# Turning edge keys by products with scaled unit matrices, and taking weight parts off in PSUM

## The chip, the cores and the metric

The kernel runs on one core of a Trainium2 chip. The metric is the device time of one execution in microseconds (us); the time shown for a version is the median of its runs.

A core has five engines with instruction queues of their own: TensorE (PE: matrix products, with PEld for loading the stationary operand), VectorE (DVE), ScalarE (ACT), GpSimd (POOL) and SyncE (SP). Here SP starts most transfers and POOL the indirect ones.

## The reference

The input is a graph of 2048 nodes with 256 features and 67584 weighted edges, sorted by dst. First a sparse product is added to x, then a layer of experts:

```python
edge_index = jnp.stack([src, dst])
x = x + _L0_gnn_ref(_layernorm(x, axis=-1), edge_weight, edge_index, node_vec1)
x = x + _L0_ffn_ref(_layernorm(x, axis=-1)[None], Wr, br, ln_g, ln_b, W1, b1, W2, b2)[0]
# _L0_gnn_ref(x, values, indices, bias):
row, col = indices[0], indices[1]                  # src, dst
gathered = values[:, None] * x[col]
return jax.ops.segment_sum(gathered, row, num_segments=2048) + bias
```

`_L0_ffn_ref` routes each token to the best two of 8 experts (256 to 1024 to 256, exact GELU) and adds their results with the softmax weights. All of it is float32.

## The kernel before

**Edge stage (0 to about 216 us).** The adjacency matrix is built densely, transposed, as 16 column blocks, and multiplied with the normalized x. The 2048 dst nodes are cut into 1024 groups of two (`GC = 2`); 128 groups, one on each partition, are a *set*, and there are 8 sets (`GQ`). For each group the kernel finds where its edges begin (`count_before`, `find_blocks`) and loads a window of 128 edges: `win_s` (src), `win_d` (dst) and `win_w` (weight), by three indirect transfers of POOL in `get_win`. In a window the group lies on the partition and the edge in the row. The products need it turned, so each set has a key step:

- `low_key` (L260) on DVE: `b_i` = src >> 7 and `f[:, 0]` = src - 128 * b_i, the src within its block of 128.
- `scale_dst` (L270) on ACT: `cl` = 16 * (dst - first dst of the group). `keys_of` (L275) on DVE adds: `f[:, 1]` = cl + b_i. This second key names a dst of the group and a block of src in a number from 0 to 31; edges of other groups fall outside it.
- `turn_key` (L280): PE transposes one key into a third of the PSUM tile `pk` (one buffer), ACT copies it as bf16, each value twice, to `k2`. It is done for key 0 and for key 1. `turn_weights` (L288) does it for the weights, whose bf16 copy is the first part of `w2`.
- `next_part` (L307), twice a set: DVE subtracts the last part of the weight from what was left (`r`), ACT copies that as bf16 to the next place of `w2`. Three bf16 parts together stand for an f32 weight.
- `count_own` on ACT counts the edges that were covered.

Each set is then worked off in four *half-batches* of 32 groups; there are 32 of them, n = 0 to 31. For half-batch n DVE makes the one-hot matrices: `make_hl` (hl, 128 wide, from key 0), `make_eq` and `make_hr` (eq, 32 wide, from key 1, and hr = eq times the three weight parts). `make_cols` (L345) makes 96 bf16 products of them on PE into `pa` (three PSUM buffers), ACT copies two tiles `ar` out, SP writes them to DRAM and, after every second half-batch, loads a column block `ac` back. From n = 8 on, `dense` (L368) multiplies finished column blocks with xn on PE, and `add` on DVE adds the result to `acc` one half-batch later. In between stands the layer norm of x (`turn_x`, `weigh_x` on PE for n up to 8, the rest on ACT).

The whole stage is in a block whose order is written out by hand for every engine: each engine executes its instructions in the order of the program text. For half-batch n this order is (L483 on): hot matrices of n + 1 on DVE, with `next_part` of a new set around them where n = 2 or n % 4 == 2; `count_before` on ACT; the keys of set q + 1 on DVE (for n = 1 and n % 4 == 0); `get_win`; adds; `make_cols(n)`; `dense`; `turn_keys`; `scale_dst`; `weigh_x`, `turn_x`; work on x. The buffers of hl and hr are two, so DVE can write those of n + 1 only when PE has finished half-batch n - 1. `k2` and `w2` have three buffers, `prep`'s tiles (b_i, f, cl, r1, r2) two.

The constants at the beginning (L112 on) stand outside that block; a scheduler places them.

**Expert stage (216 us to the end).** A branch at L588 closes the edge stage. Then come routing and slots of 256 rows through the experts, mostly on PE, and the copy of the result to the output.

Of the kernel before, what the change touches and what calls it, by code (L numbers as in the profile page):

```python
# [10 lines left out]
F32 = mybir.dt.float32  # L11
BF16 = mybir.dt.bfloat16
F16 = mybir.dt.float16
I32 = mybir.dt.int32
AF = mybir.ActivationFunctionType
OP = mybir.AluOpType
# [6 lines left out]
P = 128  # L23
# [4 lines left out]
def kernel(  # L28
# [30 lines left out]
    nc = tc.nc  # L59
# [26 lines left out]
    NU = NF + NE  # L86
    DX = D + NE
    RW = D + 4
    AHEAD = 2
    EARLY = 3  # L90

    consts = ctx.enter_context(tc.tile_pool(name="consts", bufs=1))
# [71 lines left out]
    nc.vector.memset(ones, 1.0)  # L164
    iota_b = consts.tile([P, P], BF16, name="iota_b")
    nc.vector.tensor_copy(iota_b, iota_p)
    jp = consts.tile([P, P], I32, name="jp")
    nc.gpsimd.iota(jp, pattern=[[1, P]], base=0, channel_multiplier=-1)
    before = consts.tile([P, P], BF16, name="before")
# [30 lines left out]
    wins = [None] * GQ  # L200
# [18 lines left out]
    def get_run(q):  # L219
        runs[q] = find.tile([P, EJ], I32, name="run", bufs=3)  # L220
        nc.gpsimd.indirect_dma_start(
            out=runs[q],
            out_offset=None,
            in_=dst.rearrange("(p j) -> p j", p=P),
            in_offset=bass.IndirectOffsetOnAxis(ap=blk_i[:, q:q + 1], axis=0),
        )
# [33 lines left out]
    def low_key(q):  # L260


        b_i = prep.tile([P, P], I32, name="b_i")
        nc.vector.tensor_scalar(b_i, wins[q][0], 7, None, op0=OP.arith_shift_right)
        f = prep.tile([P, 2, P], F32, name="f")
        nc.vector.scalar_tensor_tensor(f[:, 0, :], b_i, -float(P), wins[q][0], op0=OP.mult,
                                       op1=OP.add)
        return b_i, f

    def scale_dst(q):  # L270
        cls[q] = prep.tile([P, P], F32, name="cl")
        nc.scalar.activation(cls[q], wins[q][1], AF.Identity, bias=col16[:, q:q + 1],
                             scale=float(NB))

    def keys_of(q):  # L275
        b_i, f = low_key(q)
        nc.vector.tensor_tensor(f[:, 1, :], cls[q], b_i, OP.add)
        return f

    def turn_key(q, f, i):  # L280
        if i == 0:
            parts[q] = (keys.tile([P, 2, P, 2], BF16, name="k2"), None,
                        ps_k.tile([P, 3, P], F32, name="pk"))
        k2, _, pk = parts[q]
        nc.tensor.transpose(pk[:, i, :], f[:, i, :], ident)
        nc.scalar.copy(k2[:, i], pk[:, i, :, None].to_broadcast([P, P, 2]))

    def turn_weights(q):  # L288
# [18 lines left out]
    def next_part(q, i):  # L307

        k2, w2, rest = parts[q]
        r = prep.tile([P, P], F32, name=f"r{i}")  # L310
        nc.vector.tensor_tensor(r, rest, w2[:, :, i - 1, 0], OP.subtract)
        nc.scalar.copy(w2[:, :, i, :], r[:, :, None].to_broadcast([P, P, 2]))
        parts[q] = (k2, w2, r)

# [68 lines left out]
    with tc.manual_schedule(engines=ALL):  # L383
# [7 lines left out]
        def turn_x(j):  # L391

            t = ps_s.tile([P, 2, 512], F32, name="py1")
            pt = t[:, 0, :].rearrange("p (b r) -> p b r", r=P)
            for i in range(2 * KD):
                b, k = 2 * j + i // KD, i % KD
                nc.tensor.transpose(pt[:, i, :], acc[:, b, k * P:(k + 1) * P], ident)
            xT = prep.tile([P, 2 * KD, P], F32, name="xT")
            nc.scalar.copy(xT, pt)  # L399
            turned[j] = xT, t  # L400
# [55 lines left out]
        get_run(1)  # L456
        get_run(2)
        get_run(3)
        scale_dst(0)
        b_i, f = low_key(0)  # L460
        turn_key(0, f, 0)
        nc.vector.tensor_tensor(f[:, 1, :], cls[0], b_i, OP.add)
        turn_key(0, f, 1)
        hl = make_hl(0)
        turn_weights(0)
        next_part(0, 1)
# [16 lines left out]
        for n in range(NH):  # L483
            q = n // 4
            new = 1 if n == 2 else q + 1 if n > 4 and n % 4 == 2 and q + 1 < GQ else None
            if n + 1 < NH:
                hl = make_hl(n + 1)
                if new is not None:
                    next_part(new, 1)
                hots[n + 1] = hl, make_hr(n + 1, make_eq(n + 1))  # L490
                if new is not None:
                    next_part(new, 2)
            f = None
            if n == 1:
                fq = 1
                f = keys_of(1)
            if n % 4 == 0 and q + 2 < GQ:
                count_before(q + 2)
            if n % 4 == 0 and q and q + 1 < GQ:
                fq = q + 1  # L500
                f = keys_of(fq)
            elif n % 4 == 1 and q + 2 < GQ:
                get_win(q + 2)
                if q + 4 < GQ:
                    get_run(q + 4)
            if n in (5, 8, 11, 14):
                b = 4 * (n // 3 - 1)
                scales_x(slice(b, b + 4))
            if n in (7, 10, 12, 14):
                b = {7: 0, 10: 4, 12: 8, 14: 12}[n]  # L510
                weigh_n(slice(b, b + 4))
            for p in late:
                add(*p)
            late = []
            make_cols(n, *hots.pop(n))
            g, k = divmod(n - NB // 2, NB // 2)
            if g >= 0:
                late.append(dense(GROUPS[g], 2 * k))
            if f is not None:
                turn_keys(fq, f)  # L520
            if n == 0:

                tr = ps_k.tile([P, 3, P], F32, name="pk").rearrange("p a b -> p (a b)")
                nt = NE * KH + 2 * NE * KD + NB
                cols = consts.tile([P, nt], F32, name="cols")
                o = 0
                for rows in (b1_rows, g_rows, be_rows, nv_rows):
                    m = rows.shape[0]
                    nc.tensor.transpose(tr[:, o:o + m], rows, ident[:m, :m])
                    o += m  # L530
                for k in range(KD):
                    nc.tensor.matmul(tr[:, nt:nt + NE], ones, wr_sb[:, k, :], start=(k == 0),
                                     stop=(k == KD - 1))
                nc.scalar.copy(cols, tr[:, :nt])
                nv_c = cols[:, NE * (KH + 2 * KD):]
                by_e = consts.tile([P, NE, KH + 2 * KD], F32, name="by_e")
                o = 0
                for lo, m in ((0, KH), (KH, KD), (KH + KD, KD)):
                    nc.vector.tensor_copy(by_e[:, :, lo:lo + m],
                                          cols[:, o:o + NE * m].rearrange("p (e n) -> p e n", n=m))  # L540
                    o += NE * m
                nc.sync.dma_start(cols_d.rearrange("e p c -> p e c"), by_e)

                wc = consts.tile([P, KD, NE + 1], F32, name="wc")
                nc.vector.memset(wc[:, :, NE:], 1.0)
                nc.vector.scalar_tensor_tensor(
                    wc[:, :, :NE], tr[:, None, nt:nt + NE].to_broadcast([P, KD, NE]), -1.0 / D, wr_sb,
                    op0=OP.mult, op1=OP.add)
            if n % 4 == 3 and q + 2 < GQ:
                scale_dst(q + 2)  # L550
            if n == 0:
                scale_dst(1)
            if 1 <= n < 9:
                weigh_x(n - 1)
            if n < 8:
                turn_x(n)
            for m, work, j in X_WORK:
                if m == n:
                    work(j)
            if n == 12:  # L560

                less_m = small.tile([P, NB], F32, name="less_m", bufs=1)
                nc.vector.tensor_tensor(less_m, less, nv_c, OP.subtract)
                nc.sync.dma_start(xr_d[N:, :].rearrange("(t p) c -> p t c", p=P),
                                  none[:, None, :].to_broadcast([P, TT, RW]))
                nc.sync.dma_start(y_d[N:, :].rearrange("(t p) d -> p t d", p=P),
                                  none[:, None, :D].to_broadcast([P, TT, D]))
            if n == NH - 3:
                used = small.tile([P, 1], F32, name="used", bufs=1)
                nc.vector.tensor_reduce(used, used_q, AX.X, OP.add)  # L570
                used_i = small.tile([1, 1], I32, name="used_i", bufs=1)
                pu = ps_k.tile([P, 3, P], F32, name="pk")[:, 0, :1]
                nc.tensor.matmul(pu, ones, used, start=True, stop=True)
                nc.vector.tensor_copy(used_i, pu[0:1, :])
# [624 lines left out]
```

## Time and profile before

| | |
|---|---|
| median of 3 runs | 511.28 us (511.26 to 512.25) |
| profiled execution | 512.25 us, its span 510.5 us |
| PE busy | 462.3 us (91%) |
| PEld busy | 394.0 us (77%) |
| DVE busy | 278.2 us (54%) |
| ACT busy | 200.4 us (39%) |
| POOL busy | 154.7 us (30%) |
| hl (L320) on DVE | 32 of 2285 ns |
| hr (L335) on DVE | 32 of 1758 ns |
| products into pa (L359) on PE | 3072, 61.3 us |
| dense products (L373) on PE | 512, 121.3 us |

The profile shows one execution. Its span runs from the first to the last instruction. Products on PE overlap, so the length of one says less than the distance of two starts. A profile line of a single instruction has its start and its length in us, engine, line, operation, output and inputs with their shape, and in brackets how long the engine stood idle before it and what it waited for. PEclk is the clock that TensorE was granted, 1.00 for full speed.

### The profile page before, as it was taken

What the parts mean: (1) busy time and instruction counts of PE and PEld (TensorE: products, weight loads), DVE (VectorE), ACT (ScalarE), POOL (GpSimd) and SP (SyncE); (2) the same over time, 40 slices, a digit from 0 to 9 for tenths busy, and PEclk for the clock granted to TensorE, in tenths of its full rate; (3) what the DMA queues carried; (4) which work ended last, traced back from release to release, by engine and by line L of the source; (5) the groups of instructions that cost most, each with busy time, mean ns of one, the idle gap of its engine ahead of it and who ended that gap; (6) DMA issues with size and microseconds to landing.
All of it is one profiled execution on the core that took longest, in us unless ns stands there. A gap on an engine that the chain in (4) does not pass through costs nothing.

```text
span 510.5 us, 12148 instructions
## 1 busy us (share of the span) xinstructions
PE 462.3 (91%) x4996; PEld 394.0 (77%) x4996; DVE 278.2 (54%) x575; ACT 200.4 (39%) x489; POOL 154.7 (30%) x127
## 2 busy tenths in 40 slices
PE   1669989898999999899999999999999999996993
PEld 0557877676787887788878888888888888886882
DVE  5879899999999984347656122334332222121011
ACT  2355768662433221058272333332333333332220
POOL 5650506133040000000342433554334334422221
PEclk9999789999999999999999999999999999999898
DMA  3755577777656665991514996799998767739421
GB/s 111 221 166 163 189 219 239 219 215 242 212 172 190 202 183 172 346 322 67 163 41 104 342 339 173 233 347 365 349 342 263 208 157 205 217 90 319 139 88 35
DMA packets 87684, 106.82 MB, mean 209 GB/s; under 512 B 8656, under 2 KB 77376, under 8 KB 85504
## 3 DMA queue, kind: packets, MB, share of 16 engines
q1 hardware_dynamic: 79632, 92.08, 55.1%
q0 software_dynamic: 7952, 13.77, 11.3%
q8 instruction: 44, 0.72, 0.6%
q14 instruction: 24, 0.20, 0.1%
q10 hardware_dynamic: 32, 0.04, 0.0%
HBM read 79.85 MB, written 28.14 MB: 212 GB/s over the span
## 4 chain that ended last, share of the span: by engine, by line
PE 43%; DMA 10%; issue 2%; DVE 1%; SPq 0%; POOL 0%; POOLq 0%; ACT 0%; DVEq 0%
PE py L1030 18%; PE ph L1016 17%; DMA xs<-xr_d,to_i 7%; PE py L373 4%; PE px L843 2%; DMA out<-y_d 2%; PE px L981 1%; DMA y_rows<-out,to_i 1%; DMA out<-ys,to_i 0%; PE listed L824 0%; SPq L1168 0%; POOL out L1051 0%; POOLq L1195 0%; DVE in_hi L816 0%; DVE in_lo L810 0%
## 5 line engine op out<-in xcount | busy, mean ns | idle before, releaser
L1016 PE MATMUL ph<-xeT,w 128*128 128x256 f32 (+1 forms) x576 | 123.7, 371 | 5.6 <-PEq L1156 4.0
L1016 PEld LDWEIGHTS ph<-xeT,w 128*128 128x128 f32 x576 | 105.0, 192 | 20.3 <-issue 6.3
L1030 PE MATMUL py<-w,hT 128*128 128x256 f32 x544 | 120.6, 379 | 0.0
L1018 ACT ACTIVATE hT<-ph,ec 128x256 f32<-128x256 f32 (+1 forms) x144 | 65.9, 462 | 137.0 <-PE ph L1016 73.9
L1030 PEld LDWEIGHTS py<-w,hT 128*128 128x128 f32 x544 | 102.0, 190 | 13.2
L373 PE MATMUL py<-xn_lo,ac 128*128 128x264 f32 x352 | 85.1, 394 | 0.0
L1038 POOL DMA_INDIRECT y_d<-ys,to_i x30 | 48.9, 1631 | 114.7 <-DVE ys L1033 80.8
L320 DVE TENSOR_TENSOR hl<-k,iota_b 128x4096 bf16<-128x4096 bf16 x32 | 73.1, 2285 | 4.4 <-PE pa L359 2.2
L373 PEld LDWEIGHTS py<-xn_lo,ac 128*128 128x128 f32 x352 | 65.2, 191 | 12.5 <-ACT ar L362 0.2
L359 PE MATMUL pa<-hl,hr 128*32 128x128 bf16 x3072 | 61.3, 241 | 10.1 <-DVE hr L335 5.6
L359 PEld LDWEIGHTS <-hr 128*32 128x32 bf16 x3072 | 52.5, 108 | 21.7 <-issue 13.3
L1033 DVE SCALAR_TENSOR_TENSOR ys<-py,wt,b2w 128x256 f32<-128x256 f32 x34 | 16.4, 483 | 80.2 <-PE py L1030 65.6
L948 POOL DMA_INDIRECT xs<-xr_d,to_i x40 | 41.9, 1047 | 52.5 <-DVE r L714 32.8
L335 DVE TENSOR_TENSOR hr<-eq,w 128x3072 bf16<-128x3072 bf16 x32 | 56.3, 1758 | 2.5 <-ACT xT L399 0.5
L990 DVE TENSOR_SCALAR xeT<-px,ec 128x256 f32<-128x256 f32 (+1 forms) x38 | 18.4, 526 | 62.9 <-PE px L981 55.3
L362 ACT COPY ar<-pa 128x512 f32<-128x512 f32 x64 | 35.6, 585 | 31.7 <-PE pa L359 22.2
L240 POOL DMA_INDIRECT win_s<-in_src,at_i x8 | 11.3, 1418 | 87.9 <-DVE at_i L236 70.4
L378 DVE TENSOR_TENSOR acc<-acc,py 128x528 f32<-128x528 f32 x37 | 25.8, 700 | 22.2 <-PE py L373 22.2
L373 PE MATMUL py<-xn_hi,ac 128*128 128x264 f32 x160 | 36.2, 387 | 1.4 <-DVEq L588 1.4
L373 PEld LDWEIGHTS py<-xn_hi,ac 128*128 128x128 f32 x160 | 30.2, 190 | 6.8 <-issue 1.8
L1005 ACT ACTIVATE b2w<-b,wt 128x256 f32<-128x256 f32 x36 | 16.3, 500 | 27.9 <-DVE wt L1003 25.6
L327 DVE TENSOR_TENSOR eq<-k,iota_b 128x1024 bf16<-128x1024 bf16 x32 | 21.9, 683 | 0.0
(205 smaller groups left out, 336.3 us busy)
## 6 DMA issues: line engine op xcount, KB each, us to landing
w<-in_L_ffn_W SPq DMA_DIRECT2D x44, 1024.0 KB
ad<-ar SPq DMA_DIRECT2D x32, 512.0 KB
ac<-ad SPq DMA_DIRECT2D x16, 1024.0 KB
b<-in_L_ffn_b SPq DMA_DIRECT2D x22, 128.0 KB
acc<-in_x SPq DMA_DIRECT2D x4, 512.0 KB
out<-y_d SPq DMA_DIRECT2D x4, 512.0 KB
xr_d<-rec SPq DMA_DIRECT2D x1, 1300.0 KB
y_d<-acc SPq DMA_DIRECT2D x1, 1280.0 KB
```

Of the source, the lines that this page charges most:

```text
L320: nc.vector.tensor_tensor(hl.rearrange("p g (n t) -> p g n t", t=2), two(k2[:, 0], g, P), pair(P), OP.is_equal)
L327: nc.vector.tensor_tensor(eq.rearrange("p g (n t) -> p g n t", t=2), two(k2[:, 1], g, RK), pair(RK), OP.is_equal)
L335: nc.vector.tensor_tensor(hr.rearrange("p g i (n t) -> p (g i) n t", t=2), eq[:, :, None, :].to_broadcast([P, GH, 3, RK]), w[:, :, None, : ...
L359: nc.tensor.matmul(pa[j * RK:(j + 1) * RK, m, :], hr[:, g, i, :], hl[:, g, :], start=(i == 0), stop=(i == 2), tile_position=(0, j * RK))
L362: nc.scalar.copy(ar[:, m0:m0 + 4, :], pa)
L373: nc.tensor.matmul(pa[:, i, :DX], acs[c][:, b + i, :], xn(c), start=(c == blocks[0]), stop=(c == blocks[-1]))
L378: nc.vector.tensor_add(acc[:, b:b + 2, :], acc[:, b:b + 2, :], pa[:, :, :DX])
L948: nc.gpsimd.indirect_dma_start(out=(sets[s.set][0] if into is None else into)[:, t, :], out_offset=None, in_=(xr_d if rows is None else ro ...
L1016: nc.tensor.matmul(ph, w1[:, k, c * P:(c + 1) * P], xeT[:, k, :], start=(k == 0), stop=(k == KD - 1))
L1018: nc.scalar.activation(hT[:, c, :s.n * P], ph, AF.Gelu, bias=ec[:, c:c + 1], scale=1.0)
L1030: nc.tensor.matmul(py, hT[:, c, t * P:(t + 1) * P], w2[:, c, :], start=(c == 0), stop=(c == KH - 1))
L1038: st = nc.gpsimd.indirect_dma_start(out=y_d[:, :], out_offset=bass.IndirectOffsetOnAxis(ap=tos[s.to][:, t:t + 1], axis=0), in_=ys, in_offs ...
```

## The change

The low key becomes src & 127, cast to f16 as `lo` (by DVE for set 0, by ACT for the others). ACT makes f16 copies of src (`s_h`) and of the scaled dst (`cl`). DVE no longer computes b_i or either sum. Instead of transposing, PE multiplies the f16 tiles with `turns`, three unit matrices scaled by 1, 1/128 and -1/128, which turns and scales at once: key 0 is lo turned; key 1 is cl + s_h / 128 - lo / 128, three products added up in PSUM.

For sets 0 to 3 (`q < SOON`), `next_part` builds what is left of the weight in PSUM: it turns the window of weights again by an f32 product with the unit matrix and takes off the earlier parts by products with -1 times a unit matrix (`less_b`). DVE's subtraction goes, ACT's copy stays and reads PSUM. For sets 1 to 3 the two calls move in the program: the first after `make_cols(n)`, the second after `turn_x(n)`. Sets 4 to 7 keep the subtraction on DVE. In `turn_key` the order of ACT's work for set 0 changes too: key 0 is copied out before `scale_dst`.

```diff
+    SOON = 4
...
+    turns = consts.tile([P, 3, P], F16, name="turns")
+    for i, c in enumerate((1.0, 1.0 / P, -1.0 / P)):
+        nc.vector.tensor_scalar(turns[:, i, :], ident, c, None, op0=OP.mult)
+    less_b = consts.tile([P, P], BF16, name="less_b")
+    nc.vector.tensor_scalar(less_b, ident, -1.0, None, op0=OP.mult)
...
     def low_key(q):
-        b_i = prep.tile([P, P], I32, name="b_i")
-        nc.vector.tensor_scalar(b_i, wins[q][0], 7, None, op0=OP.arith_shift_right)
-        f = prep.tile([P, 2, P], F32, name="f")
-        nc.vector.scalar_tensor_tensor(f[:, 0, :], b_i, -float(P), wins[q][0], op0=OP.mult,
-                                       op1=OP.add)
-        return b_i, f
+        lo_i = prep.tile([P, P], I32, name="lo_i")
+        nc.vector.tensor_scalar(lo_i, wins[q][0], P - 1, None, op0=OP.bitwise_and)
+        lo = prep.tile([P, P], F16, name="lo")
+        nc.vector.tensor_copy(lo, lo_i) if q == 0 else nc.scalar.copy(lo, lo_i)
+        return lo
 
     def scale_dst(q):
-        cls[q] = prep.tile([P, P], F32, name="cl")
-        nc.scalar.activation(cls[q], wins[q][1], AF.Identity, bias=col16[:, q:q + 1],
+        s_h = prep.tile([P, P], F16, name="s_h")
+        nc.scalar.copy(s_h, wins[q][0])
+        cl = prep.tile([P, P], F16, name="cl")
+        nc.scalar.activation(cl, wins[q][1], AF.Identity, bias=col16[:, q:q + 1],
                              scale=float(NB))
-
-    def keys_of(q):
-        b_i, f = low_key(q)
-        nc.vector.tensor_tensor(f[:, 1, :], cls[q], b_i, OP.add)
-        return f
-
-    def turn_key(q, f, i):
+        cls[q] = cl, s_h
+
+    def turn_key(q, lo, i):
...
-        nc.tensor.transpose(pk[:, i, :], f[:, i, :], ident)
+        terms = [(lo, 0)] if i == 0 else [*zip(cls[q], (0, 1)), (lo, 2)]
+        for m, (t, c) in enumerate(terms):
+            nc.tensor.matmul(pk[:, i, :], t, turns[:, c, :], start=(m == 0),
+                             stop=(m == len(terms) - 1))
         nc.scalar.copy(k2[:, i], pk[:, i, :, None].to_broadcast([P, P, 2]))
...
     def next_part(q, i):
         k2, w2, rest = parts[q]
-        r = prep.tile([P, P], F32, name=f"r{i}")
-        nc.vector.tensor_tensor(r, rest, w2[:, :, i - 1, 0], OP.subtract)
+        if q < SOON:
+            nc.tensor.matmul(rest, wins[q][2], ident, start=True, stop=False)
+            for j in range(i):
+                nc.tensor.matmul(rest, less_b, w2[:, :, j, 0], start=False, stop=(j == i - 1))
+            r = rest
+        else:
+            r = prep.tile([P, P], F32, name=f"r{i}")
+            nc.vector.tensor_tensor(r, rest, w2[:, :, i - 1, 0], OP.subtract)
         nc.scalar.copy(w2[:, :, i, :], r[:, :, None].to_broadcast([P, P, 2]))
...
+        lo = low_key(0)
+        turn_key(0, lo, 0)
         scale_dst(0)
-        b_i, f = low_key(0)
-        turn_key(0, f, 0)
-        nc.vector.tensor_tensor(f[:, 1, :], cls[0], b_i, OP.add)
-        turn_key(0, f, 1)
+        turn_key(0, lo, 1)
...
-                if new is not None:
+                if new is not None and new >= SOON:
                     next_part(new, 1)
                 hots[n + 1] = hl, make_hr(n + 1, make_eq(n + 1))
-                if new is not None:
+                if new is not None and new >= SOON:
                     next_part(new, 2)
...
-                f = keys_of(1)
+                f = low_key(1)
...
             make_cols(n, *hots.pop(n))
+            if new is not None and new < SOON:
+                next_part(new, 1)
...
                 turn_x(n)
+            if new is not None and new < SOON:
+                next_part(new, 2)
```

More of the change, by code (lines that the diff above doesn't have):

```diff
@@ L500 @@
                 fq = q + 1
-                f = keys_of(fq)
+                f = low_key(fq)
             elif n % 4 == 1 and q + 2 < GQ:
```

## The prediction

> **What bounds the kernel now.** First the chain that ended last: from 215.82 us to the end it is matmuls of TensorE and, at the tail, DMA landings. Nothing there is touched by the change, so whatever the edge stage (0 to 215.8 us) gains or loses arrives at the end one for one. The question is what bounds that stage, and the slices of the page show two engines near full in it:
>
> ```profile
> PE   1669989898999999899999999999999999996993
> DVE  5879899999999984347656122334332222121011
> PEclk9999789999999999999999999999999999999898
> ```
>
> A slice is 12.8 us. DVE (row 2) is at 9 from slice 6 to 13, but so is PE. So I read who waits for whom. In 56 to 118 us (us in total, times, longest):
>
> ```profile
> PE pa L359 <- DVE hr L335: 1.1, 1, 1.1
> PE pk L285 <- DVE f L266: 0.6, 2, 0.4
> ...
> DVE hl L320 <- remote: 2.1, 1, 2.1
> ```
>
> DVE waits once, at its head (55.82 us, for half-batch 5 on PE), and PE waits for DVE 1.7 us in all. In 118 to 195 us neither waits for the other: PE is busy 75.09 of 77 us and keeps 5.21 us a half-batch, 22.5 us for four with their key turn; DVE needs 22.3 us. So DVE's work is worth at most those 1.7 us of PE's waiting after 56 us, unless PE also gets quicker. After 118 us, PE alone sets the pace.
>
> Before 56 us the two take turns. PE waits 2.5 us for f of set 1 (28.66 us); then DVE waits 1.9 us for half-batch 2 (37.65), 0.3 for half-batch 3, 2.1 for half-batch 5. So between 28.7 and 55.8 us the path runs over PE, and PE is slow there: half-batch 4 (96 products) takes 2.75 us, half-batch 9 only 1.52. The clock by windows (columns: window, length, busy PE, PEld, DVE, ACT, POOL with counts, then PEclk, DMA share, GB/s):
>
> ```profile
> 52.10:55.50 3.40, 3.40 (x94) 3.20 (x83) 1.58 (x5) 1.83 (x6) 1.45 (x2) 0.50 0.32 96
> 55.50:58.90 3.40, 3.40 (x83) 3.07 (x87) 3.08 (x3) 2.23 (x9) 3.10 (x2) 0.50 0.52 158
> ...
> 62.30:65.70 3.40, 2.22 (x61) 1.80 (x48) 3.30 (x5) 3.40 (x13) 0.00 (x0) 1.00 1.04 361
> 65.70:69.20 3.50, 3.48 (x98) 3.19 (x99) 3.46 (x4) 3.14 (x9) 0.00 (x0) 0.51 0.68 207
> ```
>
> PE ran at half clock from 52.1 to 58.9 and again from 65.7 to 69.2 us, each time after a stretch in which it was a third idle (busy 2.34 of 3.40 us in 48.7 to 52.1, 2.22 in 62.3 to 65.7). Before 48 us the column says 1.00, but the durations say half; I call such stretches cold.
>
> Last, the step the change rewrites, in time order (start, length, engine, line), here for set 5:
>
> ```profile
> 115.72 0.22 DVE L264 TENSOR_SCALAR b_i<-win_s 128x128 int32<-128x128 int32 x1
> 115.98 0.29 DVE L266 SCALAR_TENSOR_TENSOR f<-b_i,win_s 128x128 f32<-128x128 int32 x1
> 116.19 0.28 DVE L277 TENSOR_TENSOR f<-cl,b_i 128x128 f32<-128x128 f32 x1
> 116.32 0.33 PE L285 MATMUL pk<-ident,f 128*128 128x128 f32 x1 [0.39 <-DVE f L266]
> 116.39 0.70 DVE L378 TENSOR_TENSOR acc<-acc,py 128x528 f32<-128x528 f32 x1
> 116.69 0.37 ACT L286 CAST k<-pk 128x256 bf16<-128x256 f32 x1 [3.86 <-PE pk L285]
> ```
>
> DVE gives PE the first key, PE turns it, ACT copies it out; the next turn waits for that copy (0.46 us each time). Starts, not lengths, show what DVE pays: 0.26 + 0.21 + 0.20 = 0.67 us.
>
> **The change, part by part.**
>
> *Four constants.* In the order of DVE's instructions they stand ahead of diag. Such instructions start 0.13 us apart (4.28, 4.41, 4.55, 4.68), so diag is 0.5 us later. The first at_i, which now has 0.2 us of waiting for ACT, comes 0.3 later, and with it POOL's window loads and, 0.3 to 0.5 later, its three run loads; get_x on SP, behind find_blocks, comes 0.5 later.
>
> *Set 0.* ACT copies the low key before it scales dst, so hl(0) starts about 0.1 to 0.4 us earlier; no gain, since hr(0) waits for the weight parts. These went DVE 0.32, ACT 0.41, twice; now each DVE step is an f32 product with 1 or 2 bf16 ones on a cold PE. The row for an f32 product at 128x128 is L450: two passes, 0.80 us. So hr(0) ends 1.2 to 1.8 us later. Cover: after it DVE waits 1.00 us for the sign of run 1 (17.31 us, a DMA landing, itself 0.3 to 0.5 later). If the landing did not move, nothing would cover it. I take half-batch 1 on DVE at +0.5 (0.3 to 0.8).
>
> *Keys of sets 1 to 7.* DVE: 0.67 to 0.25 us, a gain of 0.41 a set. ACT: lo and s_h are new. No row has int32 to f16; cl and own, from int32, take 0.40 us, plain f32 copies of this size 0.25 to 0.41: I take 0.40 for its type. s_h is in a place where ACT idles (it waited 5.1 us for win_d before cl of set 1). But lo is queued in ACT ahead of the two ar copies of make_cols (1.05 us together), and it waits for DVE, which does lo_i only after hr(n+1). Behind it wait both ar copies, then k, then PE's next turn. From DVE's start of the step to k: 0.25 + 0.1 + 0.40 + 1.05 = 1.8 us instead of 0.97 (115.72 to 116.69). That is +0.8 us where PE is not already later than that (sets 4, 5), less where it is (set 2 +0.5, sets 3 and 6 +0.3, set 7 +0.1). PE: three 16-bit products for the second key. Rows: pa, bf16, 0.22 us alone and 0.016 in a row; f32 turn 0.33. So between -0.1 and +0.2 us a set; I take 0, nearest to one latency of 0.22 plus two short steps.
>
> *Weight parts of sets 1 to 3.* DVE: two starts of 0.24 (147.00 to 147.24, 149.63 to 149.87), -0.49 a set. PE gets two f32 and three bf16 products. Nearest row: four f32 one-pass turns of x (L397) take 0.64 us warm and 1.09 cold, 0.16 or 0.27 a pass. Two products of two passes: 0.64 or 1.09; three bf16 at 0.08 to 0.13: 0.9 us warm, 1.5 cold. Bounds: 0.5 from the dense rows (264 columns in 0.235 us, scaled) and 2.9 if each stood alone as L450 does. ACT's copies stay; the second waits for PE, but hr that needs it is an iteration away.
>
> *The sum*, along the path. Set 1: DVE starts it at 27.97 + 0.5, k is at 30.27 instead of 29.15: +1.1. Half-batch 2 then carries the parts of set 1, cold: +1.3 (under the 1.5, since weighing and turning x hide the last latency), of which I let 0.6 vanish in the gaps that PE has there anyway (two of 0.3 put down to "issue"): half-batch 3 at +1.8. hl(5) waits for it, so lo of set 2 too: 47.70 + 1.8 + 1.8 = 51.3 for a k that was at 49.01: +2.3 at half-batch 5, and DVE, which waited for that one at 55.82, is +2.3 too. Half-batch 6: PE +0.9 for set 2, less the 1.08 us it waited for hr(8): +2.1 at half-batch 8 (DVE +1.8, the gain of its two subtractions). Set 3: k at 70.28 + 1.8 + 1.8 = 73.9 against 71.84, no more than PE's own lateness. Half-batch 10: +0.9. Sets 4 and 5: PE's waits for f (0.19 and 0.39) go, as DVE by then is only +0.5 (1.8, less 0.41 each for the keys of sets 3 and 4 and 0.49 for the parts of set 3). So 2.1 + 0.9 - 0.6 = **+2.4 us**, carried to the end. DVE's 1.8 us of savings in this stretch buy only a longer lead. What is late next is PE, everywhere.
>
> The profiled execution took 512.25 us for a span of 510.50 us, 1.75 around it: it would become 514.65. It was the slowest of three; on the median of 511.28 the same shift gives **513.7 us**. Ends of this case: parts at 0.5 with all gaps swallowing them, start +0.3: about +1.0. Parts at 1.5 everywhere and start +0.8: +3.6.
>
> *A rule against the rows.* The two windows at 52.1 and 55.5 us were full of matmuls (3.40 of 3.40) and the clock stayed at 0.50 through both. The Trainium skill, "TensorE: Matmul & The Clock Gate", Part 1, says that about 3.4 us of sustained work bring the full clock, and one idle window takes it back; the second half agrees here (2.22 of 3.40, then 0.51), the first does not for 52.1. Its Part 4 says that transposes do not count as busy work as products do; no row here shows it. By that rule this change, which replaces 16 transposes by products and adds more, would be warm about one window earlier: an estimate from this page of up to 1.7 us less, a sum of +0.7 instead of +2.4.
>
> **The rivals.**
> 1. *The clock turns (faster).* If the extra products keep PE at full clock from 52.1 to 58.9, half-batch 5 costs 1.52 instead of 2.51, the weighing of x 1.06 instead of 1.88, its turn 0.63 instead of 1.09, most of half-batch 6 0.8 less: 3.1 us, so -0.8 there; then +0.9 for set 2, less the wait of 1.08, +0.9 for set 3, less 0.6 for f: -0.7. If the stretch from 65.7 stays warm too (half-batch 8 at 1.52 for 2.75, its dense part 0.3 less), another 1.5: -2.2, 509.1 us. DVE allows it: -0.8 less its savings of 1.8, plus lo's 0.8, is -1.8 at set 5, near enough. It is faster than a measurement's error only if both stretches are warm. For: PE gets more to do just there, and the 1.08 us hole ahead of the second stretch is filled in my own sum. Against: 3.40 of 3.40 did not suffice at 52.1.
> 2. *It cancels.* PE's gaps put down to "issue" (2.8 us in 56 to 118) may end at times of their own, and a later PE falls into them: +0.8 at most remains, 512.1 us. The first warm stretch alone ends here too, at 510.6.
> 3. *A longer cold stretch (slower).* Later and longer turns of set 2 leave half-batches 7 and 8 cold: 7 costs 1.0 and its x steps 1.2 more, 8 no less than now: 2.3 + 2.2 + 0.2 for a slow dense part, + 0.9 - 0.6 - 1.08 = +3.9, 515.2 us.
>
> **How the numbers follow.** Forecast 0.44, cancelling 0.14, longer cold 0.16, clock turned on both stretches 0.26. About 0.2% (1.0 us) is what a measurement can tell from no change; so slower 0.60, same 0.14, faster 0.26. The likeliest case alone spans 512.3 to 514.9 us. The range takes in rival 3, with the upper price of the parts on it, and about half of rival 1: 509.3 to 516.0, with 0.13 below and 0.05 above.
>
> **What would show it.** Right: DVE's busy time down by some 5 us and yet PE's half-batch 17 starting near 120.6 us instead of 118.16; ACT's lo with a long idle before it and both ar copies after it; DVE waiting for pa in 20 to 60 us. Wrong: PEclk at 1.00 in 52 to 59 us, half-batch 17 before 118, or the parts of a set costing PE under 0.5 us.

## The result and the profile after

The changed kernel takes 517.46 us (median of 5 runs, 516.57 to 519.69), the kernel before 511.26 us beside it (509.77 to 512.25): a ratio of 1.0136, 95% interval 1.0108 to 1.0163. It is slower, as forecast, but by 6.2 us instead of 2.4, and outside the range (509.3 to 516.0). The profiled execution took 516.57 us for a span of 514.7, against 512.25 and 510.5 before, so the two traces differ by 4.2 us in span. A ratio, here and below, is not the quotient of the two medians, and it leaves out executions that lie more than 1.5% above the fastest of their kernel.

The row of PE's slices, as shown of before:

```profile
PE   1657967988999999999999999999999999997993
```

DVE's busy time fell from 278.2 to 272.6 us, the 5 us that the change was to take off it. PE's first ten slices are emptier than before. The waits in 56 to 118 us (us in total, times, longest):

```profile
PE pa L371 <- issue: 5.9, 3, 2.6
DVE hl L332 <- PE pa L371: 5.3, 2, 3.1
```

Before, PE's gaps put down to "issue" (the engine waited for nothing that the profile shows) were 2.8 us there, in seven pieces of at most 0.7 us. Now there are three, and two of them are over 2.5 us. The timeline of PE shows where they lie; half-batches 8 and 9 after:

```profile
66.34 1.40 PE L371 MATMUL pa<-hl,hr 128*32 128x128 bf16 x86 [0.45 <-DVE hr L347]
70.28 0.51 PE L371 MATMUL pa<-hl,hr 128*32 128x128 bf16 x10 [2.53 <-issue]
70.71 4.36 PE L385 MATMUL py<-xn_lo,ac 128*128 128x264 f32 x12
...
77.43 1.47 PE L371 MATMUL pa<-hl,hr 128*32 128x128 bf16 x91
81.47 0.27 PE L371 MATMUL pa<-hl,hr 128*32 128x128 bf16 x5 [2.58 <-issue]
```

and the same two half-batches before:

```profile
65.72 2.75 PE L359 MATMUL pa<-hl,hr 128*32 128x128 bf16 x96 [1.08 <-DVE hr L335]
68.40 3.29 PE L373 MATMUL py<-xn_lo,ac 128*128 128x264 f32 x12
...
74.11 1.52 PE L359 MATMUL pa<-hl,hr 128*32 128x128 bf16 x96
```

The 96 products of a half-batch wait for the same hl and hr, so after the 86th I take it that the instructions are missing. In the window 66 to 82 us the transfers list holds two packets on a queue of its own kind (44 of them, 0.72 MB, in the whole trace, so 16 KB each):

```profile
q8 instruction: 2, 0.03, 0.7%
```

Narrowed down, one packet begins at 67.9 us and one at 79.2: each begins within 0.3 us after PE stopped, and PE goes on some 2.3 us later. Counting weight loads and products in the timeline, 252 PE instructions lie between the two gaps. I call such a gap a dry spell.

Half-batch by half-batch, the lateness of PE's column products against before was: +1.8 us at 0, +0.7 at 1, +1.4 at 3, -0.55 at 4, +2.35 at 5, +0.6 at 8, +3.3 at 9, +6.1 at 10, +5.1 at 17, +4.7 at 31. So the two dry spells carry the lateness from half-batch 8 to 10: from 8 to 9, 2.53 us, plus 1.07 for a dense part that runs slower after the gap (4.36 us for 3.29), less 0.84 for shorter busy time in half-batch 8; from 9 to 10, 2.58 and 0.2.

From the first column products to the last dense ones (17 to 240 us before, 17 to 243 after) they are not all of it. PE's issue gaps ahead of column products sum to 5.9 us, against 4.2 before; its waits for k rose from 6.1 to 8.4, and its waits for the first key of a set from

```profile
PE pk L285 <- DVE f L266: 3.1, 3, 2.5
```

to

```profile
PE pk L290 <- ACT lo L272: 7.2, 3, 4.4
```

Against this PE waited less for hr (3.8 us for 5.6), and it was busy with column products for 53.7 us instead of 61.3.

The clock by windows (window, length, PE, PEld, DVE, ACT, POOL, then PEclk, DMA share, GB/s):

```profile
53.10:56.60 3.50, 3.50 (x101) 3.17 (x101) 0.66 (x5) 2.28 (x8) 2.18 (x3) 0.51 0.87 266
56.60:60.00 3.40, 3.40 (x123) 3.01 (x114) 3.03 (x3) 2.52 (x9) 3.10 (x2) 1.00 0.58 170
...
66.80:70.20 3.40, 0.95 (x69) 0.77 (x54) 3.37 (x3) 1.52 (x6) 0.00 (x0) 1.00 0.88 268
70.20:73.60 3.40, 3.32 (x17) 2.49 (x18) 3.37 (x6) 1.27 (x3) 0.00 (x0) 0.50 0.28 55
```

Where before had 0.50 up to 58.9 us and 0.51 in 65.7 to 69.2, the clock is now full from 56.6 to 70.2: the first rival happened in part, and it is why half-batch 8 is only 0.6 us late. Then the dry spell at 67.8 us leaves PE 0.95 us of work in a window, and the next one is at 0.50.

Last, ACT and PE at the key of set 2 (start, length, engine, line):

```profile
48.72 0.30 ACT L272 CAST lo<-lo_i 128x128 f16<-128x128 int32 x1 [1.95 <-DVE lo_i L270]
48.93 1.07 ACT L374 COPY ar<-pa 128x512 f32<-128x512 f32 x2
49.08 0.23 PE L290 MATMUL pk<-turns,lo 128*128 128x128 f16 x1 [2.38 <-ACT lo L272]
49.88 0.39 ACT L292 CAST k<-pk 128x256 bf16<-128x256 f32 x1
```

In this order the prediction had it: ACT idles 1.95 us for lo_i, both ar copies come next, and k only after them. Its time was another: k came at 49.88 us, 0.9 later than before, where 2.3 was forecast.

### The profile page after: what moved, and what is told of

Same layout as the page of the kernel before. It is cut to its first block, busy times and chain, and to the rows that moved or that the text cites. A ratio compares the mean times of both kernels' runs of the same rounds, so it can differ in the third digit from the quotient of the medians.

```text
span 514.7 us, 12224 instructions
## 1 busy us (share of the span) xinstructions
PE 459.2 (89%) x5040; PEld 392.9 (76%) x5040; DVE 272.6 (53%) x556; ACT 203.6 (40%) x504; POOL 151.1 (29%) x127
## 4 chain that ended last, share of the span: by engine, by line
PE 42%; DMA 10%; issue 2%; DVE 1%; ACT 0%; SPq 0%; POOL 0%; POOLq 0%; DVEq 0%
PE py L1045 17%; PE ph L1031 16%; DMA xs<-xr_d,to_i 7%; PE py L385 4%; PE px L858 2%; DMA out<-y_d 1%; PE px L996 1%; DMA y_rows<-out,to_i 1%; DMA out<-ys,to_i 0%; PE listed L839 0%; SPq L1183 0%; ACT b2w L1020 0%; POOL out L1066 0%; POOLq L1210 0%; DVE xeT L1005 0%
## 5 line engine op out<-in xcount | busy, mean ns | idle before, releaser
L1033 ACT ACTIVATE hT<-ph,ec 128x256 f32<-128x256 f32 (+1 forms) x144 | 65.7, 461 | 137.8 <-PE ph L1031 84.4
L371 PE MATMUL pa<-hl,hr 128*32 128x128 bf16 x3072 | 53.7, 230 | 9.7 <-issue 5.9
L371 PEld LDWEIGHTS <-hr 128*32 128x32 bf16 x3072 | 47.4, 102 | 19.1 <-issue 10.4
L246 POOL DMA_INDIRECT win_s<-in_src,at_i x8 | 12.9, 1609 | 97.7 <-DVE at_i L242 47.3
```

The source lines that it names most:

```text
L371: nc.tensor.matmul(pa[j * RK:(j + 1) * RK, m, :], hr[:, g, i, :], hl[:, g, :], start=(i == 0), stop=(i == 2), tile_position=(0, j * RK))
L1033: nc.scalar.activation(hT[:, c, :s.n * P], ph, AF.Gelu, bias=ec[:, c:c + 1], scale=1.0)
```

## The experiments

Each ratio is to the kernel before on the same chip, run beside it. That kernel took 516.8 and 516.2 us in the first two sets of runs (two chips) and 511.0, 510.1 and 509.9 in the three others, so times of different sets are not set against each other, and ratios of different sets only with care.

### One half of the change each

Keys alone: SOON set to 0 in the changed kernel, so that VectorE takes off all weight parts.

```
-    SOON = 4
+    SOON = 0
```

> The changed kernel with SOON = 0: new keys on every set, weight parts all subtracted on DVE as before. Theory W (the loss is PE's and ACT's extra steps): the parts were +2.2 us of the forecast, so +0.5 to +2 us against before remain, from lo ahead of ar in ACT. Theory F (PE's instruction stream runs dry for 2.5 us where a boundary of 256 instructions falls into half-batches 8 and 9): the boundary moves by some 50 instructions towards later, out of half-batch 8's products, so the two gaps of 2.5 us on PE become small and the time is within 2 us of before; gaps put down to issue sum to under 4 us.

517.81 us, ratio 1.0036 (1.0007 to 1.0065).

Parts alone: the kernel before with less_b and the new next_part, and its calls moved as in the change.

```
+        if q < SOON:
+            nc.tensor.matmul(rest, wins[q][2], ident, start=True, stop=False)
+            for j in range(i):
+                nc.tensor.matmul(rest, less_b, w2[:, :, j, 0], start=False, stop=(j == i - 1))
```

> The kernel before with only the weight parts of sets 0 to 3 taken off in PSUM, at the changed kernel's places. W: +1 to +3 us against before, nearly all of the forecast. F: some 46 instructions of PE more ahead of half-batch 8 than before, against 54 in the changed kernel, so the boundary falls on the last 10 to 15 products of half-batch 8 again: two gaps of about 2.5 us, +4 to +6 us.

525.23 us, ratio 1.0126 (1.0056 to 1.0195; four executions). On this chip the parts seem to carry more of the loss than the keys, though the two intervals touch. Neither profile shows the two gaps of 2.5 us: with the keys alone, where I expected them to shrink, no gap is over 1.03 us, and with the parts alone, where I expected them again, none is over 1.27. Both kernels lose time in a row of short gaps between 54 and 60 us instead.

### Padding: do the gaps hang on the count of instructions?

spare(k) issues k products of 8 columns into a PSUM region that nobody reads. 27 of them (54 PE instructions) before the first column products of the kernel before; then 45 and 45 in the changed kernel, before the first and in half-batch 1:

```
+        def spare(k):
+            for _ in range(k):
+                nc.tensor.matmul(pft[:32, 1, :8], ones_b[:, :32], ones_b[:, :8], start=True,
+                                 stop=True, tile_position=(0, 0))
+        spare(27)
```

> The kernel before with 54 spare PE instructions (27 products of 32 columns by 8, into PSUM that nobody reads) while PE waits for the first hr. They add no work that anything waits for. W: no change, within 1 us of before. F: the boundaries fall where they fall in the changed kernel, 86 products into half-batch 8 and about 89 into half-batch 9, with gaps near 2.5 us each, and the time is 2 to 6 us longer than before.

> The changed kernel with 180 spare PE instructions, 90 while PE waits for the first hr and 90 while it waits for lo of set 1. W: no change against the changed kernel or up to 2 us slower (the spare products run into the first half-batch). F: the boundaries of half-batches 8 and 9 move ahead of their products, into the work on x; the two gaps of 2.5 us go or shrink, half-batch 10 starts 3 to 5 us earlier, and the time is 2 to 5 us shorter than the changed kernel's.

The first: 518.85 us, ratio 1.0037 (1.0009 to 1.0065). The second: 528.6 us, ratio 1.0196 (1.013 to 1.0262), the opposite of what I expected. The gaps moved in both, but not to where my count put them. In the padded kernel before, PE is fed in drops at half-batch 5, with POOL's window loads and the rest of the traffic beside it:

```profile
52.24 2.00 PE L359 MATMUL pa<-hl,hr 128*32 128x128 bf16 x66
54.42 0.37 PE L359 MATMUL pa<-hl,hr 128*32 128x128 bf16 x5 [0.18 <-issue]
55.18 0.40 PE L359 MATMUL pa<-hl,hr 128*32 128x128 bf16 x6 [0.39 <-issue]
...
58.79 0.43 PE L359 MATMUL pa<-hl,hr 128*32 128x128 bf16 x8 [1.03 <-issue]
```

Five products come every 0.75 us where 66 took 2.0, and the half-batch takes 6.9 us. So products that do almost nothing cost 1.9 us in the one kernel, and in the other the issue gaps within the column products add up to 10.5 us, against 4.2 in the first trace of the kernel before.

The two kernels once more on another chip, and with other pads (32 in the changed kernel; 45 and 19 in the one before):

> The kernel before, unchanged, with a profile beside the other runs of this set. Theory F (PE runs out of instructions at places set by how its instruction blocks fall on the work, worst while POOL starts the window loads): the time is the one the kernel before shows on this chip, and the excess of the products of half-batches 1 to 16 over 1.52 us (2.75 cold), 6 us in the first profile, is larger by about as much as the time is longer than 511. Theory W (extra steps): nothing to say.

> The changed kernel, unchanged, on the same chip. W: +2.4 to +6 us against before on any chip. F: the steps of the change are worth about +2.5 us, the rest is where the gaps fall, so the difference to before on this chip may be anything from 0 to +8 us, and the profile's gaps account for what differs from +2.5.

> The changed kernel with 64 spare PE instructions (32 small products) while PE waits for the first hr. W: within 1 us of the changed kernel. F: the gaps sit elsewhere and the time differs by 2 us or more, in either direction.

> The kernel before with 128 spare PE instructions, 90 while PE waits for the first hr and 38 while it waits for f of set 1. W: within 1 us of before. F: differs by 2 us or more from before or from the version with 54, and as its gaps differ.

Before again: 516.23 us, 1.0007 (0.9969 to 1.0045). After again: 521.19 us, 1.0072 (1.0029 to 1.0116). After with 32: 521.08 us, 1.0084 (1.0046 to 1.0121). Before with 64: 517.5 us, 1.0016 (0.9994 to 1.0037). On this chip the kernel before has dry spells of its own (1.19 and 1.18 us in half-batch 6), and the change costs less against it. These pads changed neither kernel's ratio beyond the noise, where I had expected 2 us or more if the count decides. Padding shifts every later instruction, but I could not steer it.

### The order of the key step

ACT's copy of lo behind both ar copies (it moves from low_key into turn_keys); and lo_i and lo of sets 2 to 7 ahead of hl(n+1):

```
     def turn_keys(q, f):
+        f, f_i = f
+        nc.scalar.copy(f, f_i)
```

> The changed kernel with ACT's copy lo of sets 1 to 7 moved in the program to just ahead of the first turn, so that it stands in ACT behind both ar copies instead of ahead of them. Theory L (PE waits longer for lo and for k because lo holds up ACT): PE's wait for k falls from 3.6 us to the 1.9 of before in 26 to 118 us, and the time is 1 to 2 us under the changed kernel's, so +3 to +4 against before. Theory S (the parts' extra PE steps carry the loss): no change, +5. Theory F (gaps of the instruction stream): either, with gaps that account for it.

```
+            f = None
+            if n % 4 == 0 and q and q + 1 < GQ:
+                fq = q + 1
+                f = low_key(fq)
             if n + 1 < NH:
                 hl = make_hl(n + 1)
```

> The changed kernel with lo_i and lo of sets 2 to 7 made ahead of hl(n+1), a half-batch's DVE work (4.7 us) earlier; set 1 stays. L: PE no longer waits for lo of set 2 (2.4 us in the first profile) nor, beyond 0.46 a turn, for k; 2 to 3 us under the changed kernel's time, +2 to +3 against before. S: no change, +5. F: either, with gaps that account for it.

Behind ar: 520.85 us, ratio 1.0191 (1.0147 to 1.0235). Early: 518.68 us, ratio 1.0152 (1.0106 to 1.0198). Neither recovers anything, though PE's wait for lo in 26 to 118 us fell to one of 2.7 us in the second. By itself that would say that the key's order does not matter; the next two runs say that it does, once the parts are out of the way. The kernel before with its b_i and both sums moved ahead of hl(n+1) in the same way, and the changed kernel with SOON = 1:

> The kernel before with b_i and both sums of sets 2 to 7 made ahead of hl(n+1) on DVE, nothing else. If waits for the key bound PE also before the change: PE's waits for f and ar ahead of the turns of sets 2 to 7 (2.3 to 2.6 us where they stood in the second set of profiles) go, 1 to 3 us less than before. If PE's own work and gaps bound it: within 1 us.

> The changed kernel with SOON = 1: new keys everywhere, weight parts in PSUM for set 0 only, those of sets 1 to 3 on DVE as before. S: the two f32 and three bf16 products a set cost 0.9 to 1.5 us each for three sets; about 2 to 3 us under the changed kernel, +2 to +3 against before. L: no change against the changed kernel, +5. F: either, with gaps that account for it.

Before with early keys: 508.23 us, ratio 0.9940 (0.9914 to 0.9967), faster than both kernels. SOON = 1: 513.95 us, ratio 1.0059 (1.0037 to 1.0081). With early keys PE waits for hr instead of f, and its issue gaps are small:

```profile
PE pa L359 <- DVE hr L335: 5.1, 7, 1.1
...
PE pa L359 <- issue: 0.7, 1, 0.7
```

Half-batch 5 starts at 46.1 us instead of 51.8, half-batch 17 at 112.9 instead of 118.2. With SOON = 1 the parts of sets 1 to 3 are gone from PE, and so are the long gaps ("issue" 0.5 us in 26 to 118), while PE's wait for lo is the longest of all (7.8 us, four times; 3.1 for f before). That kernel keeps one of the two costs and loses the other.

### Count, work or place

Four runs on one chip: the changed kernel again; the kernel before with 7 spare products in the places of the parts of each of sets 1 to 3 (the count alone); with the very products of those parts, read by nobody (count and work); and the changed kernel with SOON = 0 and early keys.

> The changed kernel unchanged, to stand beside the three others on one chip. Both theories: 1.007 to 1.014 of the kernel before (as measured so far on two chips), gaps of TensorE put down to issue of 4 us or more in half-batches 0 to 8.

516.38 us, ratio 1.0111 (1.0083 to 1.0138).

```
+        for _ in range(2 + i):
+            nc.tensor.matmul(idle[q][:32, 0, :8], ones_b[:, :32], ones_b[:, :8], start=True,
+                             stop=True, tile_position=(0, 0))
```

> The kernel before with 7 spare products of 8 columns (14 TensorE instructions, some 0.3 us, nothing waits for them) after the column products of half-batches 2, 6 and 10, as many instructions as the parts of sets 1 to 3 take in the changed kernel. Theory C (the count of instructions decides, through where the supply of instructions runs dry): +2 us or more, with gaps in other half-batches than before. Theory W (the work and the waits of the parts decide): no more than +0.7 us, a ratio under 1.0015.

510.41 us, ratio 1.0000 (0.9982 to 1.0018).

```
+        out = idle[q][:, 0, :]
+        nc.tensor.matmul(out, wins[q][2], ident, start=True, stop=False)
+        for j in range(i):
+            nc.tensor.matmul(out, iota_b, w2[:, :, 0, 0], start=False, stop=(j == i - 1))
```

> The kernel before with the very products of the parts of sets 1 to 3 (two f32 and three bf16 of 128x128 a set) on TensorE in the places where the changed kernel has them, written into a used PSUM region; nothing waits for them and VectorE still subtracts. Theory W: TensorE's 0.9 us warm and 1.5 cold a set, in all +2 to +3.3 us. Theory C: the same as the run with the spare products, within 1 us of it. If it stays under +1 us, then neither the work nor the count, but the order on ACT and the waits for the parts carry the loss.

510.89 us, ratio 1.0021 (1.0002 to 1.0040).

> The changed kernel with SOON = 0 (all parts subtracted by VectorE again) and lo_i and lo of sets 2 to 7 ahead of hl(n+1). If the new keys cost nothing once they are early, it comes to the time of the kernel before with its keys early, a ratio of 0.994 (some 508 us where before is 511). If the turning by products costs by itself (three products for one turn, ACT's lo and s_h), 1.000 or more.

508.2 us, ratio 0.9966 (0.9951 to 0.9981). So the work of the parts of three sets costs about 0.2% (1.1 us) in the kernel before, and the count alone nothing: the simple form of the theory that the count decides is out. The new keys, once early, cost next to nothing against the old ones (0.9966 against 0.9940, with intervals that overlap).

That leaves a contradiction: early keys are at 0.9966 without parts in PSUM and at 1.0152 with them. The last two runs take it apart: early keys with SOON = 1, and early keys with all subtractions on VectorE and the products of sets 0 to 3 on PE beside them, read by nobody. The second has the same PE instructions in the same order as the kernel at 1.0152.

```
+    def idle_part(q, i):
+        _, w2, _ = parts[q]
+        out = idle[q][:, 0, :]
+        nc.tensor.matmul(out, wins[q][2], ident, start=True, stop=False)
+        for j in range(i):
+            nc.tensor.matmul(out, less_b, w2[:, :, 0, 0], start=False, stop=(j == i - 1))
```

> Early keys as before, and only the parts of set 0 in PSUM. The start is 1.8 us later at hr(0); the prediction let only 0.5 us of it reach half-batch 1. If the start costs what it shows there, 1.8 us over the kernel with early keys alone: a ratio of about 1.000. If cover takes it, 0.997 to 0.998. Then the rest of the 1.0152 lies with sets 1 to 3.

> Early keys, VectorE subtracts all parts, and TensorE has in addition the products of the parts of sets 0 to 3, into a used PSUM region that nothing waits for: the same TensorE instructions in the same order as the early-keys kernel with the parts in PSUM (1.0152). Theory C (the stream decides): TensorE's long issue gaps come back at the same instructions (n = 6, 9 and after 17, 2.7 to 3.9 us each) and the ratio is 1.010 or more. Theory W (the waits decide): no issue gap over 1.8 us, and the ratio is below 1.003.

SOON = 1: 507.47 us, ratio 0.9955 (0.9938 to 0.9973): with early keys the parts of set 0 in PSUM cost nothing, and all of the loss is with sets 1 to 3. Idle products: 514.12 us, ratio 1.0059 (1.0027 to 1.0091). The timeline of PE, the idle products' gaps first, then those of the kernel that it copies:

```profile
56.32 0.80 PE L379 MATMUL pa<-hl,hr 128*32 128x128 bf16 x43 [1.74 <-issue]
67.19 0.34 PE L379 MATMUL pa<-hl,hr 128*32 128x128 bf16 x10 [1.97 <-issue]
78.18 0.27 PE L379 MATMUL pa<-hl,hr 128*32 128x128 bf16 x5 [3.77 <-issue]
104.48 0.85 PE L379 MATMUL pa<-hl,hr 128*32 128x128 bf16 x46 [0.77 <-issue]
...
126.51 4.52 PE L393 MATMUL py<-xn_lo,ac 128*128 128x264 f32 x12 [3.06 <-issue]
```

```profile
54.84 1.36 PE L371 MATMUL pa<-hl,hr 128*32 128x128 bf16 x43 [2.70 <-issue]
66.80 0.34 PE L371 MATMUL pa<-hl,hr 128*32 128x128 bf16 x10 [0.62 <-issue]
76.96 0.27 PE L371 MATMUL pa<-hl,hr 128*32 128x128 bf16 x5 [3.13 <-issue]
103.49 0.85 PE L371 MATMUL pa<-hl,hr 128*32 128x128 bf16 x46 [1.00 <-issue]
125.80 4.17 PE L385 MATMUL py<-xn_lo,ac 128*128 128x264 f32 x12 [3.88 <-issue]
```

The gaps stand ahead of the same instructions: the last 43 products of half-batch 6, the last 10 of 8, the last 5 of 9, the last 46 of 14, the last 12 products of the dense part after 17. The changed kernel has three of them, ahead of the same 10, 5 and 46, and so has its repeat, which is shown here:

```profile
68.10 0.34 PE L371 MATMUL pa<-hl,hr 128*32 128x128 bf16 x10 [2.05 <-issue]
78.03 0.27 PE L371 MATMUL pa<-hl,hr 128*32 128x128 bf16 x5 [1.21 <-issue]
103.07 0.85 PE L371 MATMUL pa<-hl,hr 128*32 128x128 bf16 x46 [0.84 <-issue]
```

The gap ahead of the last 10 was 2.53, 2.05, 2.34, 0.62 and 1.97 us in five profiles of this stream (the changed kernel, its repeat, lo behind ar, lo early, idle products). In these five, neither the waits nor the order of the other engines moved the places where PE runs dry; how long it stands there differs.

The chip or the execution does move them. The changed kernel on the chip of the second set is the same program, and there the gap ahead of the last 10 is 0.57 us, and half-batch 9 has none:

```profile
74.65 0.34 PE L371 MATMUL pa<-hl,hr 128*32 128x128 bf16 x10 [0.57 <-issue]
...
80.57 3.04 PE L371 MATMUL pa<-hl,hr 128*32 128x128 bf16 x96
```

Half-batch 5 comes in drops instead (6.8 us), no gap is over 0.6 us, and the ratio is still 1.0072.

What ends a gap is told by the list of packets. In the first two traces and the ten of the last three sets, 38 gaps of over 0.5 us are put down to "issue", and each of them ends 2.2 to 2.5 us after the start of a 16 KB packet on the instruction queue; in the gaps of 2.5 us and more that packet starts 0.2 to 1.6 us after PE has stopped. So there PE waits for the next block of its instructions. Why a block is asked for so late is not shown, and the drops on the other two chips do not follow this rule: the gaps among them end 1.1 to 12 us after a packet's start.

Two things speak against the dry spells as the whole loss. Their sums do not order the kernels: 5.9 us in the changed kernel and 4.3 in its repeat, against 4.2 before; but 5.7 and 4.8 with early keys at 0.9966 and 0.9955, and 1.8 with SOON = 1 at 1.0059. And the kernel with the idle products took 510.7 to 511.5 us in five executions and 514.1 to 520.8 in the other six; its profile is of one of the longest (520.65 us), so it shows where the gaps are, and not how long they usually are, and what divides the two groups was not traced. By the ratios the stream with nothing waiting on it, its work included, makes 0.9966 into 1.0059, half of the way to 1.0152. Whether the other half is the parts' waits or longer dry spells stays open.

## Why the prediction was wrong in size

**What held.** DVE is not the bound, and its 5.6 us bought nothing. The start: half-batch 0 was 1.8 us late and half-batch 1 0.7, forecast 0.5 (0.3 to 0.8); with early keys the parts of set 0 cost nothing at the end (0.9955 against 0.9966). The order at the keys: lo waited for DVE, and k stood behind the ar copies. DVE waited for pa in 20 to 60 us (7.1 us). lo took 0.30 us where I used 0.40, which changes little.

**What came out by luck.** Half-batch 5 was 2.35 us late where 2.3 was forecast, but not on the forecast path. Half-batch 4 was 0.55 us early, on a warmer clock, so PE reached the key of set 2 early and stood 2.38 us for lo. Its k was 0.9 us late, not 2.3; the rest came after it, as weighing and turning x took 1.72 and 1.09 us where they had taken 0.96 and 0.64.

**What the clock gave back.** The warm clock of the first rival came true on most of its two stretches (from 56.6 us): half-batch 6 took 1.52 us where it had taken 3.07 with its gap, and half-batch 8 was 1.5 us earlier than my +2.1. Then the gap at 67.8 us ended it.

**The steps that failed** are two. The first is the credit that the sum set against the new keys. Without the parts of sets 1 to 3 it comes to nothing: 1.1 us for the start and set 1 and 0.5 for set 2, less the 1.08 of PE's wait for hr(8) and the 0.6 of its waits for f. SOON = 1 in the changed kernel is just that, and it measured 1.0059, some 3.0 us (1.9 to 4.1); the keys alone measured 1.0036, 1.8 us. The waits did not go. In the changed kernel PE still waited 0.45 us for hr(8) and 0.40 for lo of set 5, where 0.39 for f was to vanish, and for k of sets 4 and 5 it waited 0.81 and 1.01 between the turns where it had waited 0.46.

The second is the term for the parts of sets 1 to 3, 2.5 us in the sum (1.3 less 0.6, and twice 0.9). I priced them by their own length: 1.5 us cold and 0.9 warm, of which 0.6 would vanish in PE's gaps. In the changed kernel they took 0.77 and 0.88 in half-batch 2, 0.48 and 0.76 in 6 (with a wait of 0.56 for ACT's w between them), 0.48 and 0.65 in 10: 4.0 us, and 0.56, against 3.3. That was not far off, and read by nobody the same products cost 1.1 us (0.2%) in the kernel before. But what they cost depends on what stands around them: on top of SOON = 1 they bring 1.0059 to 1.0111 or 1.0136, 2.7 to 3.9 us; with early keys 0.9955 to 1.0152, about 10 us.

What I had wrong there is what the gaps are. I took PE's "issue" gaps as holes at times of their own, which a later PE falls into, in the sum and in the second rival alike, so that they could only make the change cheaper. They are places where PE runs out of instructions, and added instructions move these places: those of half-batch 2 did go, and two others came. In the kernel before, the worst in 56 to 118 us was 0.7 us. In the new stream two fell near the ends of half-batches 8 and 9, and cost 2.5 us each in the first profile (2.05 and 1.21 in the repeat), with 1.07 more for the dense part on a colder clock. The sum had no term for this, and none of the rivals had it either. That 96 short products in a row use up instructions fastest, and that the gaps are long there for this reason, was only argued, and the 3.88 us gap among dense products after half-batch 17 speaks against it as the whole reason.

How the loss divides stays open. By the ratios, the keys as placed are 0.36% alone and 0.59% with set 0's parts, and the parts of sets 1 to 3 add 0.5 to 0.8% with the keys late and 2.0% with the keys early; but these come from different sets of runs, and on the first chip the parts alone measured 1.26%.

**The rule on the clock.** Before, two windows full of products stayed at 0.50 (52.1 to 58.9 us). In the changed kernel one was enough: PE was busy all of 53.1 to 56.6 at 0.51, and the next window was at 1.00. So the rule fits the second case and not the first, and no run shows what makes the difference. I wrote that its second half agrees here; but the window that brought the clock down was a third idle, not idle (busy 2.34 of 3.40 us in 48.7 to 52.1), so these rows show a clock that falls sooner than the rule has it.

## What to carry to other kernels

When an engine issues thousands of short instructions, look for "issue" gaps amid products that wait for nothing, and for an instruction packet that starts a fixed time before they end (here 2.2 to 2.5 us): an edit that adds instructions ahead of such a stretch moves the gaps, and the range must allow for one that lands badly (here 2 to 5 us). To find out whether an added product costs by its work, its waits or its place in the stream, run it with its result read by nobody, in the same order. And try the order first: moving the key step of the kernel before ahead of hl(n+1) brought 0.6%, where a rewrite that took 5.6 us off VectorE lost 1.4%; the rewrite with only set 0's parts in PSUM and the keys early came to 0.9955, no better than the reordering alone.

## What the hardware showed that I had not expected

- PE stands still in the middle of independent products, for 0.2 to 3.9 us; where it stood over 0.5 us on the chips of the first and the last three comparisons, it went on 2.2 to 2.5 us after the start of a packet on the instruction queue. The packets of the changed kernel come 3.4 to 11.2 us apart between 45 and 131 us; 252 PE instructions lie between two gaps. The Trainium skill, "Runtime: NRT & Kernel Launch", section "Instruction fetch mechanics", gives blocks of 16 KiB, 256 instructions, which agrees with that count; it calls the cost of crossing from one to the next mostly hidden, and these runs do not agree: 2.53 and 2.58 us here, 3.88 with lo early.
- The supply can also come in drops, 5 products every 0.75 us, for a whole half-batch (6.9 us for 96 products).
- The same kernel took 510 to 511 us in four comparisons and 516 in two, on other chips. On one of those two it shows gaps of 1.19 and 1.18 us, against 0.70 at most in the same stretch of the trace of before.
